# A transformer block on one core: four PSUM banks for scores and two for transposes in place of three and three

## The chip, the cores and the metric

The kernel runs on one core of a Trainium2 chip. It is one program of some 42,500 instructions on five engines: TensorE (PE in the profile, with PEld for its weight loads), VectorE (DVE), ScalarE (ACT), GpSimd (POOL) and SyncE (SP), which issues nearly all DMAs. The metric is the device time of one execution in microseconds (us); less is better. PSUM, into which TensorE writes, has eight banks of 128 x 512 f32 values here, and all eight are given out by the lines that are changed.

## The reference

One block: attention with rotary embedding and a causal mask, then a feed-forward network whose weights come as 4-bit codes with scales. The input is 2048 x 1024 in f32, with 16 heads of 64, and the inner size of the feed-forward part is 2752. Cut to what matters:

```python
h = layernorm(x)
q, k, v = h @ Wq, h @ Wk, h @ Wv                 # 16 heads of 64
q, k = rotary(q), rotary(k)
logits = where(causal, q @ k.T, -1e9) / 8
o = softmax(logits) @ v
x = x + layernorm(o @ Wo)
h = layernorm(x)
Wg, Wu, Wd = (NF4[codes] * scales for each)      # blocks of 64
x = x + layernorm((silu(h @ Wg.T) * (h @ Wu.T)) @ Wd.T)
```

## The kernel before

Numbers that must keep f32 precision are split into a high and a low part, and a product is made of two or three matmuls (mm3, L110 to L115: hi x hi, hi x lo, lo x hi). The split itself (split, L117 to L119) is a copy on ScalarE (L118) and a subtraction on VectorE (L119). Both read the source; when that source is a PSUM bank, the bank is free once the subtraction has ended.

The work is staged:

1. **Start.** make_x loads rows of x, normalizes them, transposes them in blocks of 128 x 128 on TensorE (transposed, L146 to L155: four transposes into one bank with the tag T at L151, then two splits), and qkv makes the first projections for the first two pairs of heads. With ramp set, two of the three outputs of qkv go to a bank with the tag S and one to F.
2. **Attention.** Heads are worked on in pairs, and for each head the 2048 queries in four groups J of 512. For one (head, J), scores makes 4 (J + 1) tiles of up to 128 x 512: two matmuls into a bank with the tag S (L268, L270), a row maximum on VectorE (L276, or L274 on the diagonal, which also masks), an exponential on ScalarE (L278, with a read of the accumulated sum), and a scaling by the reciprocal sum on GpSimd (L300). The results stand in buffers with the tag pa (prob), of which there are six. Then weighted goes over 4 J + 4 blocks of 128 keys: up to four transposes of prob into a bank with the tag T (L310), a split into pw (L118, L119), and two matmuls into the one bank with the tag O (L314, L315). So there are as many score tiles as key blocks, 640 each; the diagonal ones are narrower. The projections of later heads (group, qkv) are laid between: three tiles of 24 matmuls each per group, and a function pace ties the first matmul of each tile to a point in the progress of the scores, so that they are spread over 85% of a pair's scores.
3. **Output projection, residual, second normalization**, the first four row groups beside the end of attention. The normalized rows are stored, loaded again and transposed once more (fill_x2, again with T banks and L151). Outputs of project go to F, or to F and S in turn (L454).
4. **Gate and up**, with the weights looked up from codes on ScalarE and VectorE one step ahead, and the results combined for seven products. Banks are taken in rotation over all eight (any_bank, L83 to L85).
5. **Down**: seven products of a one-level Strassen scheme, each in eight banks taken in the same rotation, with the last normalization and the stores.

Banks are kept by tag. A tag has a number of buffers, and a new tile of the tag takes the place of an older one once that one's last reader is done:

```python
BANKS = {"F": 1, "S": 3, "T": 3, "O": 1}
BANK_ORDER = ("F", "S", "S", "S", "T", "T", "T", "O")
def bank(tag, name="bk"):
    return ps.tile([P, 512], F32, tag=tag, name=name, bufs=BANKS[tag])
def any_bank():
    turn[0] += 1
    return bank(BANK_ORDER[turn[0] % 8])
```

The order of the instructions on each engine is not the order of the source. A planner at build time goes through the program with modelled durations: on each engine it takes the earliest instruction of the source among those that it holds to be ready, and an instruction that needs a new tile is ready only when a buffer of the tag is free. A few parts are given an earlier place by hand (early). The number of buffers of a tag thus acts twice: on the order that is planned, and on the waits at run time, where each engine goes through its own list strictly in order.

## Time and profile before

| What | Before |
|---|---|
| Time, median of 3 runs | 3039.47 us (3035.39 to 3045.34) |
| Time of the profiled execution | 3038.32 us |
| Its span, first to last instruction | 3036.5 us |
| PE busy | 2918.4 us (96% of the span) |
| DVE / ACT / POOL busy | 2033.8 / 1699.7 / 955.5 us |
| Mean granted TensorE clock | 0.988 of full speed |

The profile is one execution, and times in it count from its first instruction. Attention lies roughly between 152 and 1511 us, gate and up between 1690 and 2570 us. "A <- B" behind a wait names the tile written and the tile read, or the instruction waited for; L118 is line 118 of the listing. A wait on a bank is shown as a wait for the instruction that read the bank last. PE's matmuls overlap in the pipeline: one of 512 columns is shown as 0.39 us long, but the next can start 0.23 us after it. The granted clock is the share of TensorE's full speed that the chip allows at that time.

### The profile page before, as it was taken

Reading aid. Unit: us, or ns where it says so; the run is one execution under the profiler, and the core shown is the slowest. Engines: PE = TensorE matmul, PEld = TensorE weight load, DVE = VectorE, ACT = ScalarE, POOL = GpSimd, SP = SyncE. Lnnn points to the kernel's source line nnn. Section 1 sums busy time; section 2 is a strip of 40 time slices with the busy share of each in tenths; the row PEclk is TensorE's granted clock in tenths of the full one; section 3 lists DMA queues with packets and bytes.
Section 4 is the critical chain, followed back from the end, with each engine's and each line's share of the span. In section 5 each row is a group of like instructions: output and inputs, shape, how many; then the busy total and the mean of one; then the engine's idle time right before and its main releaser. Section 6 shows DMA issues by size and latency. Waiting matters only on the chain.

```text
span 3036.5 us, 42534 instructions
## 1 busy us (share of the span) xinstructions
PE 2918.4 (96%) x14168; PEld 2409.9 (79%) x14168; DVE 2033.8 (67%) x4171; ACT 1699.7 (56%) x3569; POOL 955.5 (31%) x1055
## 2 busy tenths in 40 slices
PE   7989999999999999989989999999999999899998
PEld 6868888787877787778767888888888888788887
DVE  6567778777867777777565666776666668344347
ACT  4256667676766666676555555665555556232234
POOL 5344344443444443453322122222221213100034
PEclk9999999999999999999999999999999999999999
DMA  8787666656557557472356344444433445644446
GB/s 292 270 264 233 205 212 196 192 191 205 155 193 200 191 169 229 137 241 81 104 191 215 122 139 135 152 137 134 143 122 130 137 138 180 215 136 152 146 146 232
DMA packets 271740, 536.01 MB, mean 177 GB/s; under 512 B 22944, under 2 KB 113056, under 8 KB 255648
## 3 DMA queue, kind: packets, MB, share of 16 engines
q1 hardware_dynamic: 269344, 529.10, 54.1%
q10 hardware_dynamic: 2176, 4.19, 0.4%
q8 instruction: 112, 1.84, 0.3%
q14 instruction: 108, 0.88, 0.1%
HBM read 371.98 MB, written 161.22 MB: 176 GB/s over the span
## 4 chain that ended last, share of the span: by engine, by line
PE 78%; DMA 9%; DVE 6%; ACT 3%; issue 2%; POOL 1%; SPq 0%; POOLq 0%; ACTq 0%; DVEq 0%
PE bk L112 13%; PE bk L114 13%; PE bk L113 13%; PE pt L310 6%; PE qkv L112 5%; PE qkv L113 5%; PE qkv L114 5%; PE o L315 4%; PE o L314 3%; PE s L268 3%; PE s L270 3%; DMA wf<-in_wq 2%; DMA xc<-xd 1%; PE pj L458 1%; PE pj L456 1%
## 5 line engine op out<-in xcount | busy, mean ns | idle before, releaser
L300 POOL TENSOR_SCALAR prob<-prob,rc 128x512 f32<-128x512 f32 (+3 forms) x640 | 406.0, 657 | 434.1 <-DVE rc L295 231.1
L113 PE MATMUL bk<-x,wt 128*128 128x512 f32 x1376 | 535.6, 389 | 0.0
L114 PE MATMUL bk<-x,wt 128*128 128x512 f32 x1376 | 535.2, 389 | 0.0
L112 PE MATMUL bk<-x,wt 128*128 128x512 f32 x1376 | 533.6, 389 | 1.1 <-ACT wt L118 0.9
L278 ACT ACTIVATE prob<-s,mxs 128x512 f32<-128x512 f32 (+3 forms) x640 | 402.5, 632 | 146.1 <-DVE mxs L276 91.5
L119 DVE TENSOR_TENSOR pw<-pt,pw 128x512 fp32r<-128x512 f32 (+3 forms) x640 | 378.3, 601 | 121.8 <-ACT pw L118 120.1
L118 ACT CAST pw<-pt 128x512 fp32r<-128x512 f32 (+3 forms) x640 | 324.1, 527 | 171.6 <-PE pt L310 141.0
L517 ACT ACTIVATE ln<-cs,bias 128x512 f32<-128x512 f32 x520 | 359.6, 716 | 108.0 <-DVE m L524 23.4
L310 PE MATMUL pt<-ident,prob 128*128 128x128 f32 x2176 | 346.1, 275 | 6.2 <-DVE pw L119 4.9
L310 PEld LDWEIGHTS pt<-ident,prob 128*128 128x128 f32 x2176 | 267.9, 142 | 61.2 <-issue 6.6
L112 PEld LDWEIGHTS bk<-x,wt 128*128 128x128 f32 x1376 | 258.2, 188 | 55.4 <-ACT wt L118 1.9
L114 PEld LDWEIGHTS bk<-x,wt 128*128 128x128 f32 x1376 | 258.3, 188 | 53.8
L113 PEld LDWEIGHTS bk<-x,wt 128*128 128x128 f32 x1376 | 258.2, 188 | 53.5
L276 DVE TENSOR_REDUCE mxs<-s 128x1 f32<-128x512 f32 x384 | 260.8, 681 | 59.4 <-PE s L270 58.0
L268 PE MATMUL s<-k,q 128*128 128x512 f32 (+3 forms) x640 | 265.0, 415 | 22.8 <-ACT prob L278 20.1
L315 PE MATMUL o<-pw,v 128*128 128x512 f32 (+3 forms) x640 | 247.3, 388 | 11.2 <-DVE pw L119 10.6
L314 PE MATMUL o<-pw,v 128*128 128x512 f32 (+3 forms) x640 | 244.2, 382 | 9.2 <-ACT pw L118 7.2
L112 PE MATMUL bk<-bt,at 128*128 128x512 f32 x616 | 239.9, 391 | 9.9 <-ACT in L585 8.2
L112 PE MATMUL qkv<-xc,w 128*128 128x512 f32 x576 | 230.9, 401 | 11.9 <-ACT w L179 6.8
L113 PE MATMUL bk<-bt,at 128*128 128x512 f32 x616 | 240.6, 391 | 0.0
L114 PE MATMUL bk<-bt,at 128*128 128x512 f32 x616 | 239.7, 391 | 0.0
L270 PE MATMUL s<-k,q 128*128 128x512 f32 (+3 forms) x640 | 235.6, 370 | 0.0
(146 smaller groups left out, 5512.8 us busy)
## 6 DMA issues: line engine op xcount, KB each, us to landing
xc<-xd SPq DMA_DIRECT2D x96, 1024.0 KB, 9.1
q<-qs SPq DMA_DIRECT2D x128, 256.0 KB, 7.0
ast<-S SPq DMA_DIRECT2D x44, 512.0 KB, 3.9
cs<-in_gu_scales SPq DMA_DIRECT2D x172, 128.0 KB, 3.2
cs<-in_gu_codes SPq DMA_DIRECT2D x86, 256.0 KB, 3.0
A<-in SPq DMA_DIRECT2D x66, 256.0 KB, 2.0
S<-in SPq DMA_DIRECT2D x66, 256.0 KB, 3.2
ast<-A SPq DMA_DIRECT2D x33, 512.0 KB, 4.5
```

The source lines that it names most:

```text
L112: r = T.matmul(o, lhsT=w[:, 0], rhs=xx[:, 0], start=first, stop=False)
L113: T.matmul(o, lhsT=w[:, 0], rhs=xx[:, 1], start=False, stop=False)
L114: T.matmul(o, lhsT=w[:, 1], rhs=xx[:, 0], start=False, stop=last)
L119: return V.tensor_tensor(lo, src, f32(hi), ALU.subtract)
L268: mm = T.matmul(s, lhsT=q[:, 0, j * P : (j + 1) * P], rhs=k[:, b:e], start=True, stop=False)
L270: T.matmul(s, lhsT=q[:, 1, j * P : (j + 1) * P], rhs=k[:, b:e], start=False, stop=True)
L278: A.activation(prob[i][:, j, : e - b], s, AF.Exp, bias=mx, scale=sign, accum_out=sums[:, j % BATCH, i : i + 1])
L300: G.tensor_scalar(p, p, rc[:, jj % BATCH, i : i + 1], 0.0, ALU.mult, ALU.add)
L310: T.transpose(pt[:, j * P : (j + 1) * P], prob[kb // 4][:, j, kb % 4 * P : (kb % 4 + 1) * P], ident)
L314: T.matmul(o[:, cs], lhsT=v[:, kb, :], rhs=pw[:, 0, cs], start=kb == 0, stop=False)
L315: T.matmul(o[:, cs], lhsT=v[:, kb, :], rhs=pw[:, 1, cs], start=False, stop=kb == nk - 1)
L517: A.activation(ln, c8, AF.Prelu, bias=bias_of[ab], scale=ab[0], alpha=ab[2])
```

## The change

The tag S gets four banks in place of three, the tag T two in place of three. In the rotation over all eight banks, the fifth place names S in place of T. F and O keep one each. No instruction is added or taken away; who uses which tag is as before: S for score tiles (and some outputs of qkv at the start and of project), T for all transposes of prob, x and the second normalized rows.

```diff
-    BANKS = {"F": 1, "S": 3, "T": 3, "O": 1}
-    BANK_ORDER = ("F", "S", "S", "S", "T", "T", "T", "O")
+    BANKS = {"F": 1, "S": 4, "T": 2, "O": 1}
+    BANK_ORDER = ("F", "S", "S", "S", "S", "T", "T", "O")
```

## The prediction

> **What bounds the kernel now.** I read the page first, then the stages, then who made TensorE (PE) wait in each, then single stretches. The page's first row and a table of stages (columns: busy time and instruction count of PE, weight loads, VectorE, ScalarE, GpSimd; then granted clock, DMA share, GB/s):

> ```profile
> PE 2918.4 (96%) x14168; PEld 2409.9 (79%) x14168; DVE 2033.8 (67%) x4171; ACT 1699.7 (56%) x3569; POOL 955.5 (31%) x1055
> ...
> 0.00:152.00 152.00, 134.18 (x642) 111.06 (x643) 91.10 (x217) 54.18 (x123) 64.76 (x70) 0.99 0.80 281
> 152.00:1511.00 1359.00, 1296.81 (x6947) 1070.57 (x6946) 1006.09 (x2555) 899.42 (x2333) 580.58 (x764) 0.99 0.60 189
> 1511.00:1690.00 179.00, 162.88 (x756) 133.53 (x755) 110.83 (x245) 98.97 (x168) 44.74 (x37) 0.96 0.57 190
> 1690.00:2570.00 880.00, 878.95 (x3876) 727.06 (x3875) 609.33 (x893) 495.13 (x773) 192.12 (x128) 1.00 0.42 137
> ```

> PE bounds everything. The change adds and removes no instruction, so it can only make or take away PE's idle time. The gate-up stage (1690 to 2570) has 1 us of that: nothing to win or lose there. Attention (152 to 1511) has 62 us, the start 18 us, the stretch around the output projection 16 us. Next, PE's waits in attention, then in the other two stages (total us, times, longest):

> ```profile
> PE s L268 <- ACT prob L278: 20.1, 32, 2.2
> PE o L315 <- DVE pw L119: 10.6, 19, 4.2
> ...
> PE pt L310 <- DVE pw L119: 4.9, 3, 2.4
> ...
> PE pt L151 <- DVE xr L119: 6.4, 4, 4.6
> ...
> PE pt L151 <- DVE x L119: 3.5, 3, 1.4
> ```

> The first row is a score tile waiting for one of the three S banks until ScalarE's exponential has read it: 20.1 us is all that a fourth bank can save of direct waits. The row of L310 is a transpose waiting for a T bank: only 4.9 us, but that is with three.

> How near the third T bank is to being needed is seen in a stretch where no projection matmul is left to fill PE. The timeline of PE, then of VectorE (start, duration):

> ```profile
> 632.27 0.60 PE L310 MATMUL pt<-ident,prob 128*128 128x128 f32 x4
> ...
> 633.40 0.60 PE L310 MATMUL pt<-ident,prob 128*128 128x128 f32 x4
> ...
> 634.86 0.60 PE L310 MATMUL pt<-ident,prob 128*128 128x128 f32 x4
> ...
> 634.75 0.68 DVE L119 TENSOR_TENSOR pw<-pt,pw 128x512 fp32r<-128x512 f32 x1
> ```

> Transposes of one key block start at 632.27; the subtraction that lets their bank go ends at 635.43. The next block but one starts at 634.86, 0.57 us earlier: it uses the third bank. With two it waits 0.57 us, or something else goes first. I paired the n-th group of L310 with the n-th subtraction of L119 over all 640 key blocks of the trace: 271 start before the bank of the block but one before is free, 264 us too early in sum, while only 6 come within 0.25 us of the third bank's release. Of the 640 score tiles, 83 start within 0.25 us of the release of their third bank; none would with four.

> **The change part by part.**

> *Fourth S bank.* A direct wait saved is worth its length, plus the clock. The longest S waits, 2.0 us at 536 and 2.2 us at 694, are each followed by a dip of the granted clock:

> ```profile
> 528.00:548.00 20.00, 16.98 (x77) 12.37 (x76) 15.72 (x51) 13.99 (x40) 8.91 (x15) 0.83 1.06 305
> 688.00:705.00 17.00, 14.49 (x57) 11.09 (x57) 9.30 (x30) 8.45 (x23) 8.21 (x13) 0.80 0.79 226
> ```

> 0.17 of 20 us and 0.20 of 17 us are 3.4 us each, 6.8 us together. So the gain lies between 0 and 20.1 + 6.8 = 27 us. I take 12: behind each of these waits ScalarE's queue is full, and the next score tile then waits for the same exponentials. These are its rows in attention:

> ```profile
> L278 ACT ACTIVATE prob<-s,mxs 128x512 f32<-128x512 f32 (+3 forms) x640 | 402.5, 632 | 146.1 <-DVE mxs L276 91.5 <-DVE mxs L274 41.1 <-PE pt L310 4.9
> L118 ACT CAST pw<-pt 128x512 fp32r<-128x512 f32 (+3 forms) x640 | 324.1, 527 | 171.6 <-PE pt L310 141.0 <-PE o L315 24.8 <-DVE pw L119 1.2
> L278 ACT ACTIVATION_READ_ACCUMULATOR prob<-s,mxs 128x1 f32 x640 | 130.9, 205 | 0.0
> ```

> There are as many score tiles as key blocks (640), so ScalarE needs 632 + 205 + 527 = 1.36 us for one of each, whatever the banks. A fourth bank lets PE run one tile further ahead of that pace and no more; somewhat under half of 27 is what I expect to stay.

> [...] Here PE was idle for 2.0 and 2.2 us, amid shorter waits, and the clock fell. [...]

> *Two T banks.* A bank is held from the first of its transposes to the end of the subtraction: over the 640 blocks of the trace 3.50 us in the mean, 2.83 in the median. Two banks let a block through every half of a hold. Where projection matmuls are at hand PE has other work; the delay costs nothing there. Without that cover it would show: I count 31 stretches of over 8 us in attention with neither a projection nor an output-projection matmul, 442 us with 285 key blocks, a block each 1.55 us. Of the 264 us of "too early", 151 lie in them. Their holds are 3.42 us in the mean and 2.86 in the median. By the median, two banks pass a block each 1.43 us: under 1.55, no loss. By the mean it is 1.71: 0.16 x 285 = 46 us. If every early start became a wait on its own it would be 151 us; that is no more than an outer bound, since a wait moves the next block too and score tiles may go in between. I take 30, nearer the mean than the median, because it is the long holds that close both banks. Queued behind a waiting transpose on PE are that block's two matmuls (L314, L315) and any score tile placed after it; behind those wait VectorE's maxima and ScalarE's exponentials. SP only sends loads and results around this, so no transfer is moved.

> [...] From 620.5 to 643.5, with one wait of 0.92 us, the clock here stayed at 1.00. [...]

> *The edges.* Transposes of x (L151) at the start and of x2 after attention use T banks as well. At the start ScalarE and VectorE take 2 x 0.37 and 2 x 0.42 us a bank and PE has nothing else: the first six groups that could be late are 9.4 us too early in sum by the same pairing, and all of the x2 groups 5.7. So 0 to 15 us; I take 4, as both stages already wait for the same subtractions with three banks (6.4 and 3.5 us) and VectorE sets the pace.

> *The rest.* The rotation over eight banks (projection, gate-up, down) still meets each bank once in eight turns. The first projections use S banks, and no wait on one stands in the start's list: 0, with a fourth bank too. The order on every engine is made anew by the planner from the first place where a bank is short, so unrelated waits (weights by L179, 6.8 us; xc from DRAM, 4.4 us) fall elsewhere: 0, plus or minus 10.

> *Sum.* The profiled execution took 3038.3 us (span 3036.5 and 1.8 around it), 1.2 under the median of the runs. 3038.3 - 12 + 30 + 4 = 3060.

> **The rivals.**

> *Faster.* The planner places transposes only when a bank is free and fills with scores from the fourth bank, so two T banks cost nothing, and the S waits go with their dips: 3038.3 - 27 + 4 = 3015. This decides if holds in the stretches without cover shrink below 2 x 1.36 = 2.7 us, ScalarE's own pace. For it: only 6 blocks touch the third bank's limit now, and the stretch at 632 to 637 holds for 2.0 to 3.2 us. Against it: the means above. 0.22.

> *A wash.* The stretches lose 12 us, as much as the S banks give, and the edges add 4: 3042. 0.15.

> *Much slower.* T waits become long enough to bring clock dips. 34 of the 271 early starts are early by 2 us or more; if half of them (17) turn into waits like those of 536 and 694, at 3.4 us of clock each, that is 58 us, with the 46 from the mean hold: 3038.3 + 46 + 58 - 12 + 4 = 3134. It needs T waits of over 2 us. 0.13.

> *The fourth bank isn't used.* A score tile also needs one of six prob buffers (tag pa). If those run out first, the 12 us are not gained: 3072. No wait on them shows in PE's list; it stays part of the forecast.

> **How the numbers follow.** My forecast, a loss of 10 to 60 us, has 0.50. About 0.3% (9 us) is what a measurement of this kernel can tell from no change. Faster by more is the first rival, 0.22; within it the second, 0.15; slower is 0.50 + 0.13 = 0.63. The range reaches into the faster case, to 3022, and at the other end to 3105, which holds the full 46 us in the stretches and 15 us at the edges with nothing gained (3099) and a first clock dip or two.

> **What would show it.** Right: PE's waits for ACT prob L278 at L268 fall below 12 us, those of L310 for DVE L119 rise from 4.9 to over 20 us (or show as waits of L314 and L315), the span from the first score to the last transposed probability grows by 15 to 25 us and the gate-up stage stays at 880. Wrong: attention gets shorter; the L310 waits stay under 10 us; or the change of time lies after 1690.

## The result, and the profile after

The changed kernel takes 3232.38 us in the median (3225.91 to 3237.76, four runs), the kernel before beside it 3039.86 us. The ratio is 1.0632, with a 95% interval from 1.0601 to 1.0662: 192 us slower. The sign was forecast, the size was not: the forecast was 3060, and the range ended at 3105.

The profiled execution has a span of 3235.5 us and a mean granted clock of 0.974. The page's first row, the same four stages (those behind attention moved by 199 us), and all PE waits of attention over 10 us, with two rows of ScalarE from the same view:

```profile
PE 3003.2 (93%) x14168; PEld 2437.8 (75%) x14168; DVE 2050.8 (63%) x4171; ACT 1697.0 (52%) x3569; POOL 955.7 (30%) x1055
```

```profile
0.00:152.00 152.00, 131.56 (x627) 108.52 (x628) 91.72 (x217) 55.80 (x122) 64.90 (x70) 1.00 0.79 280
152.00:1710.00 1558.00, 1389.90 (x7003) 1106.12 (x7002) 1025.35 (x2558) 898.33 (x2338) 585.42 (x766) 0.96 0.54 165
1710.00:1889.00 179.00, 150.00 (x679) 122.00 (x678) 101.87 (x230) 91.15 (x155) 41.70 (x36) 0.90 0.55 187
1889.00:2769.00 880.00, 878.65 (x3876) 726.79 (x3875) 606.64 (x895) 493.07 (x772) 186.78 (x124) 1.00 0.41 136
```

```profile
ACT pw L118 <- PE pt L310: 334.5, 233, 8.6
...
PE o L314 <- DVE ol L318: 41.6, 24, 7.6
...
ACT ol L317 <- DMA at<-ol: 38.1, 11, 5.3
...
PE s L268 <- ACT prob L278: 31.1, 56, 5.2
...
PE o L315 <- DVE pw L119: 25.4, 49, 5.7
...
PE pt L310 <- DVE pw L119: 22.7, 29, 1.5
...
PE o L314 <- ACT pw L118: 13.5, 10, 3.9
```

Nearly all of it is in attention. From the first score matmul to the last product with v it takes 1539.7 us, before 1343.6: +196 of the profile's 199. Gate and up is 880 us with 1 us idle, as before. ScalarE does the same 898 us of work in a stage that is 199 us longer.

Of the 196 us, 106 are idle time of PE (62.0 before, 168.1 after). The records show 24 stretches of half clock (granted 0.50) in attention, 122.9 us together, against 6 with 37.5 us. PE was idle for 25.3 us of them (6.9 before), and half of the rest gives some 34 us for the clock. Some 10 are work that now lies in this stage (39 matmuls of the output projection and 4 transposes more in its records). The other 46 or so stand as longer busy time of PE. Most of them are late starts as well, since a matmul is shown as busy for 0.39 us where the next could start after 0.23. Counted from one matmul's start to the next, against the median of its kind at full clock, about 158 of the 196 us are later starts, 29 are slower matmuls at half clock, and 9 are the added work.

The waits for a T bank (L310) rose from 4.9 to 22.7 us, but those for an S bank (L268) rose too, from 20.1 to 31.1, although S has one bank more. The largest new row of PE is a wait for ol, a buffer the change doesn't touch, and the largest of all is on ScalarE: its casts of transposed probabilities wait 334.5 us for PE's transposes, before 141.0.

One stretch shows how these hang together. The row of 875 to 912, and of the timelines PE and then ScalarE (in brackets the idle time before the instruction and what ended it):

```profile
875.00:912.00 37.00, 27.79 (x139) 20.95 (x138) 25.02 (x63) 21.97 (x61) 9.99 (x16) 0.86 0.58 180
```

```profile
889.93 0.28 PE L270 MATMUL s<-k,q 128*128 128x256 f32 x1
895.55 0.80 PE L314 MATMUL o<-pw,v 128*128 128x512 f32 x1 [5.34 <-DVE ol L318]
896.15 0.63 PE L315 MATMUL o<-pw,v 128*128 128x512 f32 x1
...
897.00 0.63 PE L315 MATMUL o<-pw,v 128*128 128x512 f32 x1
```

```profile
894.20 0.58 ACT L317 COPY ol<-o 64x512 f32<-64x512 f32 x1 [4.77 <-DMA at<-ol]
```

The last product of a head's group is copied from its O bank to ol (L317), of which there is one buffer, still being stored by SP's queue. So the copy waits, the O bank isn't free, and PE waits 5.34 us for its next product. From 896.15 the matmuls start 0.43 us apart instead of 0.23: the records show a granted clock of 0.50 from 891.1 to 901.4 us. Transposes and score tiles stand behind the waiting product on PE, casts and exponentials behind the copy on ScalarE.

Three figures from the records sum up what else is different. *Cover* below is PE's own work that stands in its list between a block's last transpose and its first product with v (L314), counted at 0.227 us per 512 columns and 0.109 per transpose; a split must fit in there, or PE waits.

| In attention | before | after |
|---|---|---|
| Cover, median; blocks of 640 under 1.5 us | 3.60; 45 | 1.91; 248 |
| ScalarE's idle time from the first to the last exponential; of it with a later exponential ready | 430; 145 us | 618; 501 us |
| Key blocks in stretches over 8 us with no projection and no other matmul beside attention's own | 202 in 325 us | 322 in 624 us |

The third row is counted more strictly than the 31 stretches of the prediction: transposes for v and x also end a stretch here. None of the three is a wait for a bank. Cover is a property of the order alone; the other two mix the order with the waits at run time.

### The profile page after: what moved, and what is told of

Same layout as the page of the kernel before. It is cut to its first block, busy times and chain, and to the rows that moved or that the text cites. A ratio compares the mean times of both kernels' runs of the same rounds, so it can differ in the third digit from the quotient of the medians.

```text
span 3235.5 us, 42536 instructions
## 1 busy us (share of the span) xinstructions
PE 3003.2 (93%) x14168; PEld 2437.8 (75%) x14168; DVE 2050.8 (63%) x4171; ACT 1697.0 (52%) x3569; POOL 955.7 (30%) x1055
## 5 line engine op out<-in xcount | busy, mean ns | idle before, releaser
L119 DVE TENSOR_TENSOR pw<-pt,pw 128x512 fp32r<-128x512 f32 (+3 forms) x640 | 381.0, 602 | 239.4 <-ACT pw L118 237.7
L118 ACT CAST pw<-pt 128x512 fp32r<-128x512 f32 (+3 forms) x640 | 331.6, 527 | 351.9 <-PE pt L310 334.5
L278 ACT ACTIVATE prob<-s,mxs 128x512 f32<-128x512 f32 (+3 forms) x640 | 399.2, 633 | 54.8 <-DVE mxs L276 41.3
L310 PE MATMUL pt<-ident,prob 128*128 128x128 f32 x2176 | 354.4, 280 | 25.2 <-DVE pw L119 22.7
L310 PEld LDWEIGHTS pt<-ident,prob 128*128 128x128 f32 x2176 | 272.8, 144 | 85.7 <-issue 16.4
L276 DVE TENSOR_REDUCE mxs<-s 128x1 f32<-128x512 f32 x384 | 261.3, 683 | 86.1 <-PE s L270 84.6
L314 PE MATMUL o<-pw,v 128*128 128x512 f32 (+3 forms) x640 | 261.3, 408 | 57.8 <-DVE ol L318 41.6
L268 PE MATMUL s<-k,q 128*128 128x512 f32 (+3 forms) x640 | 268.5, 421 | 34.1 <-ACT prob L278 31.1
L315 PE MATMUL o<-pw,v 128*128 128x512 f32 (+3 forms) x640 | 262.3, 411 | 27.9 <-DVE pw L119 25.4
```

Source lines behind the costliest of these rows:

```text
L118: A.copy(hi, src)
L119: return V.tensor_tensor(lo, src, f32(hi), ALU.subtract)
L268: mm = T.matmul(s, lhsT=q[:, 0, j * P : (j + 1) * P], rhs=k[:, b:e], start=True, stop=False)
L276: V.tensor_reduce(mx, s, AX.X, ALU.max, negate=True)
L278: A.activation(prob[i][:, j, : e - b], s, AF.Exp, bias=mx, scale=sign, accum_out=sums[:, j % BATCH, i : i + 1])
L310: T.transpose(pt[:, j * P : (j + 1) * P], prob[kb // 4][:, j, kb % 4 * P : (kb % 4 + 1) * P], ident)
```

## The experiments

Each ratio is to the kernel before, timed beside the experiment; its median lay between 3038 and 3045 us. Expected covers are those of the planned order, the tables' those of the traces. Edits shift lines: the transposes (L310) are L311 in experiment 10, L317 in 11 to 13 and 17, L316 in 9; the products (L314, L315) are L317 and L318 in 10, L309 and L310 in 11 to 13 and 17, L321 and L322 in 9. The kernels that carry an order over add 2 to every line (3 at the split in 9).

**Which half of the change: 1, 2, 3.** Two T banks alone, with the bank set free left out of attention; four T banks and two S banks; four S banks with the three T banks kept, for which the projections' F bank is merged into S.

```diff
-    BANKS = {"F": 1, "S": 3, "T": 3, "O": 1}
+    BANKS = {"F": 1, "S": 3, "T": 2, "O": 1, "X": 1}     # 1
+    BANKS = {"F": 1, "S": 2, "T": 4, "O": 1}             # 2
+    BANKS = {"S": 4, "T": 3, "O": 1}                     # 3
```

> Two T banks with the three S banks of before; the eighth bank has a tag of its own that only the rotation over all banks uses. If the missing T bank is the cause: 3200 to 3250 us, as with the change, PE waits at L310 of about 20 us and ScalarE idle in attention about 600 us. If the fourth S bank does the harm (scores run ahead, exponentials pile up): 3040 to 3100 us, and the mean wait from a maximum to its exponential falls from 5.1 us back towards 1.4.

> The mirror image: two S banks, four T banks. If what counts is that each of the two chains keeps three banks, this loses about as much as the change: 3150 to 3300 us. If only T is scarce, it is within 1.5% of 3040 us or faster.

> Three T banks, and four S banks by letting projections and scores share one tag (F is given up, its bank goes to S). If the loss comes from T: within 1.5% of 3040 us, perhaps 10 us under it where S waits go. If a fourth score bank is harmful in itself: over 3100 us.

Measured: 1 takes 3202.77 us, ratio 1.0529 [1.0508, 1.0550]; 2 takes 3169.98, 1.0428 [1.0412, 1.0444]; 3 takes 3276.74, 1.0777 [1.0761, 1.0793]. The loss by the missing third T bank is most of the change's, and the fourth S bank adds 30 us to it instead of taking some off. Of what was expected of 1, the time came and ScalarE's idle time of about 600 us, but not the row of L310: 6.9 us in place of about 20. A bank fewer costs 4 to 5% on either side. In 2 the loss is of another kind: the waits for an S bank at L268 are 93.0 us, while ScalarE's casts wait only 43.4 us for transposes. Experiment 3 came out over the 3100 us that were to speak for a harmful fourth S bank, but it tells little, since projections and scores now wait for each other's banks (L268 waits 65.7 us, and 36.7 for q from DRAM, once 25.3).

**Order or wait: 4, 5, 6, 7.** The number of banks acts on the planned order and on the waits at run time. To part the two, the program is planned twice: first with one number of banks, then with another, with every engine's list up to the end of attention tied to the first plan's.

```diff
+    for queue in order.values():              # each engine's list of the first plan
+        for a, b in zip(queue, queue[1:]):
+            dep = mybir.DependencyInfo(mybir.DependencyClass.NoSync, mybir.DependencyReason.DATA)
+            tc.add_manual_dep(traced[b], traced[a].name, dep, reason="order")
```

Experiment 4 runs the order planned for experiment 1 (three S, two T) with three and three banks; 5 runs the same order with the change's four and two. 6 and 7 change the order in another way, by the pacing of the projections (PACE 0.84 and 0.95 in place of 0.85), with three and three. In the traces of 1, 4 and 5 the matmuls, casts, exponentials and subtractions of attention stand in the same order; only the output projection beside its end lies otherwise.

> The order of every engine up to the end of attention is the one that is planned for two T banks and three S banks (as t2_alone), but it is run with three and three. If the cost is the planned order (queues that stand behind a blocked instruction), it stays above 3150 us although no transpose is ever short of a bank. If the cost is the wait for a bank at run time, it comes back below 3090 us.

> Every engine's order up to the end of attention is the one planned for three score and two transpose banks (t2_alone, 3203 us); at run time there are four and two banks, as in the change. A fourth bank can then only shorten waits for a score bank (46.5 us of L268 waits in t2_alone), it changes no order. Theory (what a bank does, it does through the order that is planned with it; the order planned for four score banks is 30 us worse, because scores run further ahead of ScalarE): 3160 to 3195, and the rows of L268 under 20 us. Rival (the fourth bank itself costs time when it is there, since more score tiles in flight delay the casts): 3215 to 3240, as the change.

> Banks as before (three and three); PACE is 0.84 in place of 0.85, which changes the planned order from the second pair of heads on, by moving projection tiles a little earlier. If any new order is several per cent worse than this one (the order before is a chance find), 3100 us or more. If it needs the scarce bank, within 1% of 3040 us.

> Banks as before; PACE 0.95, a larger move of the projections towards the end of each pair. Chance find: 3100 us or more. Otherwise within 1.5% of 3040 us.

Measured: 4 takes 3193.94 us, 1.0508 [1.0491, 1.0526]. With the third bank there, its waits are gone, yet only about 9 of 161 us come back, and the intervals of 1 and 4 overlap, so even these 9 are not clear of noise. The rows of ScalarE, S and T in experiment 1, then in 4:

```profile
ACT pw L118 <- PE pt L310: 322.7, 255, 6.8
...
PE s L268 <- ACT prob L278: 46.5, 73, 4.0
...
PE pt L310 <- DVE pw L119: 6.9, 9, 1.7
```

```profile
ACT pw L120 <- PE pt L312: 312.7, 252, 6.8
...
PE s L270 <- ACT prob L280: 46.7, 80, 4.5
...
PE pt L312 <- DVE pw L121: 1.0, 1, 1.0
```

5 takes 3189.19 us, 1.0476 [1.0460, 1.0491]: in an unchanged order a fourth S bank is worth 14 us over experiment 1, since its own waits nearly go, from 46.5 us to

```profile
PE s L270 <- ACT prob L280: 4.7, 3, 2.5
```

So in an order that is kept, the banks do little: the fourth S bank gains 14 us, the missing T bank costs about 9. Both hold for an order made for two T banks. The order of before, run with two, would show what the missing bank costs there; it was not run. The change, with the same banks as experiment 5, is 43 us slower than it, and that is again the order alone. 6 takes 3043.34 us, 1.0010 [0.9999, 1.0021]: this disturbance at least does not ruin the order before. 7 takes 3076.05, 1.0099 [1.0082, 1.0116], a worse pace, but far from 6%.

**The one ol buffer: 8.** The order of the change kept, with ol of the 12 middle heads in two buffers of the tag pb, which stand idle then.

```diff
-        ol = slot("ol", [D, 512], F32, "ol")
+        ol = slot("pb" if 2 <= h < 14 else "ol", [D, 512], F32, "ol")
```

> The changed kernel with its own order of every engine kept up to the end of attention, but the copy of the attention output (ol) of the middle twelve heads goes to the two pb buffers in place of the one ol buffer, so that ScalarE no longer waits at L317 for the store before. If this wait (38 us on ScalarE, 42 us on PE at L314) is a main part of the loss: 3190 to 3210 us. If it only stands in for other waits: within 12 us of 3232.

Measured: 3206.25 us, 1.0532 [1.0517, 1.0548]. PE's wait for ol falls from 41.6 to 26.3 us, ScalarE's wait for the store from 38.1 to 4.9, and the time by 26. A part, not the whole.

**Exponentials in front of casts: 9.** ScalarE is idle for 501 us while an exponential is ready behind a cast that waits. So, the change's order with some 600 moves of an exponential ahead of a cast, where the banks allow it:

```diff
+    if queue[to] in exps and queue[to - 1] in casts and may(queue[to], queue[to - 1]):
+        queue[to - 1], queue[to] = queue[to], queue[to - 1]
```

> The changed kernel with its own order of every engine kept up to the end of attention, but on ScalarE some 600 exponentials are moved one to four places forward, past casts of transposed probabilities that stand before them, wherever no engine can come to block another. If exponentials that stand behind a cast without its transpose are what makes the planned order slow: down by 60 us or more, to 3170 us or less, and the mean wait from maximum to exponential falls from 5.1 us below 4. If the lost time comes from PE's own order: within 25 us of 3232.

Measured: 3441.03 us, 1.1312 [1.1293, 1.1330], 209 us slower than the change, which neither forecast allowed. The mean wait from maximum to exponential is 4.8 us, not below 4. Moving exponentials ahead is no cure. ScalarE waits only half as long for transposes, but PE now waits for the casts, and the mean granted clock is 0.960, with the change 0.974:

```profile
PE o L321 <- ACT pw L121: 175.7, 156, 3.6
ACT pw L121 <- PE pt L316: 169.5, 101, 5.9
```

Delaying the chain from transpose through cast and subtraction to product costs more than earlier exponentials give. That ScalarE's idle time in front of it is only a consequence fits this, but is not shown by it.

**Cover: 10 to 13.** In 10, with three and three banks, a block's first transpose may not come before the second product of the block two before, which is about how far ahead two banks let it go (they free a bank a little earlier, at the end of that block's subtraction). In 11 (the change's banks), 12 (before's) and 13 (those of experiment 1), the source is written so that a block's products come behind the transposes of the two next blocks.

```diff
+                if j == j0 and len(done) >= 2:            # 10
+                    after(turned, done[-2])
+            waiting.append((kb, cs, pw))                  # 11, 12, 13
+            if len(waiting) > 2:
+                after(multiply(*waiting.pop(0)), turned)
```

> Three and three banks as before, but an edge of order alone puts the first transpose of each key block behind the second matmul of the block two before. Cover (the work that stands in PE's list between a block's last transpose and its first matmul, at 0.227 us per 512 columns and 0.109 us per transpose) falls from a median of 3.5 us to 1.7, and 294 blocks in place of 53 have under 1.5 us. If short cover is what the change costs: 3170 to 3240 us with every bank at hand. If it is the bank itself: within 1.5% of 3040 us.

> Four and two banks as changed, but each block's two matmuls are written after the transposes of the two next blocks, and ordered behind them on PE. Cover rises from a median of 1.9 us to 2.7; 57 blocks in place of 248 have under 1.5 us. If short cover is the cost: most of the 192 us comes back, 3050 to 3110 us. If two banks are too few at run time: stays above 3170 us.

> The same rewriting with three and three banks. Cover is nearly what it was (median 3.7 us, 23 blocks under 1.5 us in place of 53). If cover decides: 0 to 15 us faster than 3040. Otherwise no change beyond 9 us.

> The same rewriting with two T and three S banks (the eighth bank idle in attention); 78 blocks have under 1.5 us of cover. Against the run with four S banks it shows what the fourth S bank is worth once cover is restored: if it is worth its 20 us of direct waits, this is 10 to 30 us slower than that run; if it is worth nothing, within 9 us of it.

| | banks S, T | median cover; under 1.5 us | us | ratio |
|---|---|---|---|---|
| before | 3, 3 | 3.60; 45 | 3038.40 | 1 |
| 10 | 3, 3 | 1.70; 290 | 3207.30 | 1.0551 [1.0527, 1.0574] |
| 11 | 4, 2 | 2.69; 57 | 3196.78 | 1.0512 [1.0490, 1.0535] |
| 12 | 3, 3 | 3.82; 13 | 3039.07 | 1.0007 [0.9996, 1.0017] |
| 13 | 3, 2 | 2.69; 75 | 3172.79 | 1.0439 [1.0421, 1.0458] |

Experiment 10 is the clearest of the study: with all banks of the kernel before and one rule for PE's order, a loss as large as that of experiment 1 appears, with rows of the same kind:

```profile
ACT pw L118 <- PE pt L311: 290.0, 233, 6.8
...
PE s L268 <- ACT prob L278: 67.8, 79, 4.4
...
PE o L318 <- DVE pw L119: 37.5, 91, 2.7
```

But the reverse isn't so: cover restored with two T banks brings back 36 us of the change's 192 (11), and 30 of experiment 1's 161 (13). What was expected of 11 if short cover is the cost did not come; its time lies in the rival's range, over 3170 us. 12, with a little more cover than before, is no faster. 13 is 24 us faster than 11, where it was expected to be 10 to 30 slower or the same: with its own order, the fourth S bank costs time here too. In 11, what has gone are the waits of products for a split; in their place the transposes themselves now wait, and ScalarE for them:

```profile
ACT pw L118 <- PE pt L317: 287.9, 246, 5.9
...
PE o L309 <- DVE ol L328: 45.5, 29, 6.3
...
PE pt L317 <- DVE pw L119: 37.2, 69, 1.5
```

**What is left: 14 to 18.** 14 runs the order planned for 13 with three T banks. 15 is experiment 11 with ol in pb. 16, 17 and 18 go at the packing of the projections, in the change, in experiment 11 and in the kernel before: every contraction step of a projection is tied to its own point of the scores' progress, not only the first of an output.

```diff
-                if k == 0 and pace:
-                    pace(mm, n)
+                if pace:
+                    pace(mm, n + k / KE)
```

> Every engine's order up to the end of attention is the one planned for t2_deep2 (two transpose banks, matmuls behind the transposes of the two next blocks, 3173 us); at run time there are three banks for transposes. Theory (the order is what costs, also with the cover restored: transposes themselves are placed just where the simulated subtraction frees a bank, and ScalarE's casts stand in the queue waiting for them): 3140 to 3175, the casts' wait for transposes on ScalarE still over 200 us. Rival (with the cover restored, what is left is the wait for the second bank at run time, 29.7 us at the transposes' line, and what follows from it): 3040 to 3110, and that row of ScalarE back near 140 us.

> after_deep2 (four and two banks, matmuls behind the transposes of the two next blocks, 3197 us) with its own order kept up to the end of attention, but ol of the 12 middle heads in the two pb buffers. If the two losses add (36 us from the cover, 26 us from the one ol buffer): 3160 to 3180, with the 45.5 us of waits for ol down to 25. If the wait for ol only stands where another wait would take its place: 3190 to 3200.

> The kernel of the change, but every contraction step of a paced projection (3 matmuls) is tied to its own point of the pacing by scores, instead of only the first step of an output (24 matmuls). The projections then lie spread among the key blocks: in the planned order 129 key blocks instead of 335 stand in stretches without a projection; 211 instead of 248 blocks have a cover under 1.5 us. Theory (the loss comes from the order's packing of the projections: key blocks with none beside them run at ScalarE's and the casts' pace): 3090 to 3150. Rival (the short cover costs wherever it is): 3190 to 3235.

> after_deep2 (four and two banks, matmuls behind the transposes of the two next blocks, 3197 us) with each contraction step of a paced projection tied to its own point of the pacing. Planned: 126 blocks instead of 317 without a projection beside them, 67 with a cover under 1.5 us. Theory (packing and cover together are what the order lost): 3045 to 3110. Rival (two banks cost by themselves, whatever the order): 3150 to 3200.

> The kernel before (three and three banks) with each contraction step of a paced projection tied to its own point of the pacing. Planned: 150 key blocks instead of 260 without a projection beside them, cover under 1.5 us at 23 blocks. Theory (packing costs before the change too: 42 us of idle time lie in its stretches without projections): 3000 to 3030, faster than before. Rival (with three banks the pace is TensorE's own, and the finer ties only make it wait at the ties): 3040 to 3060.

| | us | ratio | ScalarE's casts waiting for transposes |
|---|---|---|---|
| 14 | 3147.22 | 1.0333 [1.0314, 1.0353] | 257.6 us, 235 times |
| 15 | 3164.71 | 1.0394 [1.0378, 1.0409] | 286.9 us, 248 times |
| 16 | 3184.21 | 1.0463 [1.0444, 1.0482] | 246.9 us, 231 times |
| 17 | 3170.20 | 1.0427 [1.0411, 1.0442] | 256.4 us, 252 times |
| 18 | 3038.53 | 0.9981 [0.9968, 0.9994] | 126.1 us, 137 times |

14: with the cover restored, the waits for a second T bank at run time cost 26 us of experiment 13's some 130; some 100 stay in the order. 15: the loss by ol and the loss of cover do add (32 us under 11). 16: spreading the projections takes 48 us off the change, less than its theory's 80 at least and more than its rival's 40 at most. Its stretches without other matmuls hold 116 blocks instead of 322, and idle time in them falls from 126 to 64 us, but outside them it rises from 42 to 64. So packing is a part. 17: on top of the cover it takes 27 more; its theory, a cure, fell, and the time lies in the range of the rival that two banks cost by themselves. Experiment 14 speaks against that rival for the most part, since the third bank there brought back only 26 us. 18: the same edit to the kernel before gains 0.2%, below what counts as a difference here, and short of the gain its theory forecast.

## Why the prediction was right or wrong

*What bounds the kernel, and where.* Right: only attention and its edges moved, gate and up stayed at 880 us with 1 us idle, and every engine has as many instructions as before.

*Fourth S bank, a gain of 12, between 0 and 27.* Right in kind as what it said of the bank: in an order that is kept it is worth 14 us (experiment 5). That 14 is so near 12 is partly luck, for that order had 46.5 us of waits at L268, not the 20.1 that the 12 came from. Wrong as a term of the sum: with its own order it costs 30 (experiment 1 against the change), and L268 waits did not fall under 12 but rose to 31.1.

*Two T banks, a loss of 30, between 0 and 46.* The sign held and the sign to look for came: L310 from 4.9 to 22.7 us. But that row doesn't carry the loss: with two T banks alone (experiment 1) it is 6.9 us, under the 10 that were to speak against the forecast, and the loss is 161. So the sign came right partly by luck. 46 was no upper bound of what two T banks cost, and neither was the outer 151. The working priced only waits for a bank at run time. In orders made for two banks these are worth 9 us (experiment 4, not clear of noise) to 26 (experiment 14); in the order of before, for which the 30 was worked out, they were not measured. About 152 come from the order that two banks make the planner write.

*The rest, "0, plus or minus 10".* This is the step that failed. It says that the order on every engine is made anew, and takes it for noise around nothing. In its place the runs show about 152 us for the order planned for two T banks (experiment 4) and 43 more for the one planned with the fourth S bank (the change against experiment 5). A transpose is planned only where the modelled subtraction has freed a bank; in the new order 458 of the 640 blocks have less cover than before and 179 more, and the median falls from 3.60 to 1.91 us. Experiment 10 shows that a rule which shortens cover can cost as much with every bank at hand; 11 and 13 show that cover is not all that the new order lost. The trace of before gave the scale. Holds of 2.83 us in the median need some cover, and of 640 blocks 45 had less than 1.5 us. I paired blocks with the release of banks, and asked who would wait; I should have asked what would be placed in front of whom instead.

*"So no transfer is moved."* Wrong as well. In the new order ScalarE's copies into the one ol buffer wait for its store for 38.1 us, before 11.8, and PE's products behind them for 41.6. Using the two pb buffers instead won 26 us.

*The edges, 4, between 0 and 15.* PE's idle time at the start went from 17.8 to 20.4 us and around x2 from 16.1 to 29.0: 15.5 us, just over the upper bound. Most of it is one wait of 11.4 us for a row that has to come back from DRAM, not a T bank. The stretch after attention's last product takes as long as before all the same (1526.6 us), as part of the output projection's matmuls now lies ahead of it; the start is 2.8 us longer.

*The rivals.* The faster one rested on the planner filling with scores where a transpose has no bank. Scores do run further ahead (in the change an exponential starts 5.1 us after its maximum, before 1.4), but two T banks did not cost nothing, and the waits for S banks did not go. The much slower one, 3134, was the nearest, and half right: drops of the clock came, 18 more for some 29 to 34 us, where it had 58. But it needed T waits of over 2 us, and the longest is 1.5. Most drops followed waits for ol, splits, score banks or the inputs of projections; in two of the 24 the longest wait ahead was one for a T bank, 1.5 and 1.1 us.

*What stays open.* With cover, packing and ol mended, singly or in pairs, the best is 3165 with two T banks (15), and 3147 with the order planned for two but run with three (14). Some 100 us of that order aren't explained. Their mark is in ScalarE's waits: its casts wait 231 to 271 times for transposes in every order planned for two T banks (but for experiment 9, where ScalarE's own list was changed) and 233 times in 10, and 137 to 166 times in the kernel before and in 6, 7, 12 and 18, which run within 1.2% of it. It is no mark of every slow order: in 2 and 3 they wait 38 and 155 times. That two banks tie each transpose to the modelled end of a subtraction on another engine, with no slack for real durations, would give this picture; it was argued, not shown. Cover, packing and ol mended all at once wasn't tried. Nor was the order of before run with two T banks: it could cost less than the planner's new order, or more. No kernel here beat the one before by more than 0.2%.

## What to carry to other kernels

Where a planner writes the order, the number of buffers of a tag is a scheduling decision before it is a resource: price what the order will lose (the slack between a producer and its consumer in the bottleneck's list), not only the waits for a buffer at run time. Take the slack that the present order has from the trace and ask how many blocks keep it with one buffer fewer. A buffer that nothing waits for may be the one that holds that slack, and one order run with two numbers of buffers parts the two effects. Better still is to do it both ways, with the old order and the new; here only the new one was run so.

## What the runs showed of the hardware

In the changed kernel the clock also dropped after shorter waits than the much slower rival asked for, which were T waits of over 2 us. In the kernel before, each of the six drops in attention had a PE gap ahead of it that had lasted 2.0 to 2.7 us when the drop came (three of the gaps went on, to 4.4 us at most). In the changed kernel six of the 24 drops had no gap over 1.3 us in the 7 us ahead, and a sum of gaps of 1.8 us in four of them.

In 15 of the 24 drops of the changed kernel the longest wait ahead was one for a bank (O, S or T).
